# An attention kernel on one core: TensorE's instructions in the order of the text, and its side work dealt out by half steps

## The chip, the core and the metric

The kernel runs on one core of a Trainium2 chip. The metric is the time of one execution on the device, in microseconds. The core's engines work side by side: TensorE (PE in the profile) multiplies matrices, VectorE (DVE) and ScalarE (ACT) work on elements, GpSimd (POOL) here only issues transfers that gather or scatter rows, and SyncE (SP) issues the other transfers. Each engine takes its instructions strictly in the order in which the built program lists them, and waits where an operand or a buffer is not there.

## The reference, cut to what matters

For each of 16 sequences of 1024 tokens and 512 channels, the reference computes a self-attention with 8 heads of 64 channels, masked by tokens, and adds it to the input:

```python
q = xt @ Wq.T                                   # xt: tokens x channels
scores = 0.125 * einsum('bhqd,bhkd->bhqk', qh, qh)
logits = (scores * cmask + (1 - cmask) * NEG) * rmask
ctx = einsum('bhqk,bhkd->bhqd', softmax(logits), qh)
out = x + transpose(ctx @ Wo.T)
```

Query, key and value are the same projection `q`. A masked key gets no weight; a masked query attends to all tokens alike, so all its outputs are one row per sequence.

## The kernel before

**Tiling.** About half of the tokens of a sequence ("batch") are active. `slots` sorts the active ones to the front, `index` turns this into row numbers, and the kernel gathers C = 544 slots of each sequence: four tiles of 128 rows (`xa`) and one of 32 (`xt`). All matrices of a batch are made of these slots; the other rows only get the mean row (`rest`).

**Work of a batch**, by function:
- `xt` (L388): four transposes of a gathered tile into a tile of the pool `pm`; `xsplit` (L351) then splits it into two float16 halves, `xh` by ACT (L358) and `xl` by DVE (L359). Both read the `pm` tile.
- `query` (L411): 12 float16 matmuls into `pm`, ACT copies them to `q` (L424), and for the second half of the columns DVE masks the last ones (L427). `qsplit` makes the float16 pair `hl`, and SP spreads it to `xx`.
- `value` (L461) and `value_tail` (L473): transposes of `q`, copied by ACT to `v` and by DVE to `tmp`; `top` and `bottom` (L499, L513): the shift of the exponent of four heads.
- `scores` (L542): four float16 matmuls of 272 columns into a two-bank tile `pss` (L580), and one exponential by ACT (L584). With `i=None` it does the last 32 rows of four heads at once (L555).
- `attend` (L589): attention times value. Each of its four matmuls of float32 data has 64 output columns (L597); the two of a pair of heads use the left and right half of the array. `i=4` adds the last 32 keys (L600).
- `recip_sums`, `recip_rows`, `norm`: the division by the row sums. The sums go through a transpose (L633), a DRAM tile `rd` and back as `rb` before DVE multiplies (L664).
- `project` (L687) with `product` (L672): 12 matmuls of 512 columns (L680), DVE adds the input (L685), GpSimd scatters the rows (L764). `rest` gathers the other rows into `xi`, adds the mean on DVE (L751) and scatters them.

Most results of TensorE pass through `pm`, which has two buffers; `pss` has two as well, and `pav` (attend) one.

**The order of the work.** `run` goes through the batches `b`. A batch has 18 steps: for each of 4 pairs of heads-pairs `p` and row tiles `i` two `scores`, and twice the `scores` of the last rows. In the same steps the kernel does the side work of its neighbours: the queries and values of batch `b+1`, the projection of `b-1`, the indices and gathers of `b+2`. This side work is a list `m` of pairs (cost, function), and a share of it, `total / N`, follows the two scores of each step:

```python
                goal = total * (st + 1) / N
                while pos < len(m) and (done + m[pos][0] / 2 <= goal or st == N - 1):
```

`attend` for a step runs some steps later (`todo`, `ready`), when its exponentials are done. `post` keeps scatters and gathers in two lines, `urgent` and `spare`, of which `issue` takes one in each step; such a transfer also waits for `self.beat`, the matmul issued last at that place (`once`).

**Who sets the order within an engine.** The text names the work, but the Tile scheduler orders each engine's instructions when the program is built, by priorities and by its own estimate of what is ready. So the order on TensorE need not be that of the text: matmuls of one `attend` may stand apart, with transposes or scores between them. `tc.high_priority` raises some helpers, and `behind` ties instructions to one that must come first.

Of the kernel before, what the change touches and what calls it, by code (L numbers as in the profile page):

```python
# [10 lines left out]
F32 = mybir.dt.float32  # L11
# [8 lines left out]
P = 128  # L20
# [5 lines left out]
DC = D // P  # L26
# [23 lines left out]
class Fast:  # L50
# [114 lines left out]

    def slots(self, b0, b1):
# [7 lines left out]
        mb = self.sb([P, B, TB], F32, "sc", 3)  # L174
        nc.vector.tensor_scalar(mb, self.mt[:, bs], 0.5, None, ALU.is_gt)
        mh = self.sb([P, B, TB], F16, "tmp", 2)
        nc.vector.tensor_copy(mh, mb)
# [32 lines left out]
    def facts(self, b0, b1):  # L210

# [17 lines left out]
        eh = self.sb([P, B], F16, "tmp", 2)  # L229
        nc.vector.tensor_copy(eh, e)  # L230
        pe = self.pm([P, B])
        nc.tensor.matmul(pe, lhsT=self.on16, rhs=eh, start=True, stop=True)
# [3 lines left out]

    def index(self, b):
        nc = self.nc
        s = self.st[b]
        ol = self.sb([P, TB, P], F16, "tmp", 2)  # L240
        lo = self.lo[:, b]
        nc.vector.tensor_tensor(ol, self.io128.unsqueeze(1).broadcast_to([P, TB, P]),
                                lo.unsqueeze(2).broadcast_to([P, TB, P]), ALU.is_equal)
# [228 lines left out]

    def value_tail(self, b, g):  # L473
# [6 lines left out]
        q = self.sb([P, 2, HG, CT], F32, "qt")  # L480
        nc.scalar.copy(q, s["q"][:, 2 * g:2 * g + 2, 512:C].unsqueeze(2).broadcast_to([P, 2, HG, CT]))
# [13 lines left out]
    def shift(self, b, g):  # L495
        self.top(b, g)
        self.bottom(b, g)

    def top(self, b, g):  # L499

        nc, s = self.nc, self.st[b]
        hs = slice(HG * g, HG * g + HG)
        wide = self.smcol[g]
        sm = wide[:, :HG]
        nc.vector.tensor_reduce(sm.rearrange("p (e h) -> p e h", h=2),
                                s["sd"][:, 2 * g:2 * g + 2, :].rearrange("p e (k h) -> p e h k", h=2), AX.X, ALU.max)
        nc.vector.tensor_tensor(sm, sm, s["sdt"][:, hs], ALU.max)
        pt = self.pm([P, P])
        nc.tensor.transpose(pt, wide, self.ident)
        m = s["m"] = self.sb([P, 1], F32, "m", 2)  # L510
        nc.vector.tensor_reduce(m, pt, AX.X, ALU.max)
# [262 lines left out]
    def last(self, b, todo):  # L774
# [8 lines left out]
        self.recip(b, 3)  # L783
# [5 lines left out]
        for i in range(4):  # L789
            self.product(s["ch"], s["cl"], slice(i * P, (i + 1) * P), pos[i], range(3))  # L790
        self.norm(b, 3)
# [8 lines left out]
    def run(self, flag):  # L800
# [32 lines left out]
        for c in range(DC):  # L833
            self.load("q", c, 0)
        self.slots(0, 2)
        self.warm(36)
        self.index(0)
# [16 lines left out]
        def index1():  # L854
            with self.behind(self.last_xs):
                self.index(1)
# [11 lines left out]
        first += value(0, 1) + [(0, L(self.value_tail, 0, 0))] + query(0, 2, 0) + g1[2:3] + query(0, 2, 1)[:1] + g1[3:4]  # L868
# [7 lines left out]
        begin = g1[4:] + [(1.5, lambda: None)] + query(0, 3, 0) + value(0, 2) + query(0, 3, 1) + value(0, 3)  # L876
        begin += [(0.3, L(self.value_tail, 0, 1)), (0, L(self.means, 0))]
# [4 lines left out]
        for b in range(B + 1):  # L882
            o, n = b - 1, b + 1
            if b == B:
                self.last(o, todo)
                break
            free, early, late = {}, ([], []), []
            if b >= 1:
                early = [(0, L(self.recip_sums, o, 3))], [(0.1, L(self.recip_rows, o, 3))]
                late = [(0, L(self.norm, o, 3))]  # L890
            if n < B:
                if b in tails:
                    free[0] = [L(self.late, o, 4)]
                    late += [(2.6, L(self.project_tail, o))]
                for x in rests.get(b, []):
                    free.setdefault(0, []).extend(L(self.late, x, j) for j in range(5, 9))
                    late += [(0, L(self.rest, x, j)) for j in range(5, 9)]
            chunk2 = [(0, L(self.norm, o, 2))] if b else []
            P_ = (lambda *i: project(o, *i)) if b else (lambda *i: [])
            tp, bt = [(0.1, L(self.top, b, 1))], [(0.1, L(self.bottom, b, 1))]  # L900
            if n < B:
                m = xt(n)[:1] + early[0] + xt(n)[1:2] + chunk2 + xt(n)[2:3] + early[1] + xt(n)[3:] + tp + query(n, 0, 0) + query(n, 0, 1) + bt + value(n, 0)
                m += query(n, 1, 0) + late + P_(0) + query(n, 1, 1) + P_(1)
                m += [(0, L(self.range_x, n, c)) for c in range(DC)]
                r = P_(2) + value(n, 1) + [(0.25, L(self.value_tail, n, 0))] + query(n, 2, 0) + query(n, 2, 1)
                r += query(n, 3, 0) + [(0.1, L(self.top, n, 0))] + value(n, 2) + query(n, 3, 1)
                r += [(0.1, L(self.bottom, n, 0))] + P_(3) + value(n, 3)
                r += [(0.25, L(self.value_tail, n, 1)), (0, L(self.means, n))]
                if b + 2 < B:
                    m += [(0.5, L(self.index, b + 2))]  # L910
                    r[1:1] = [(0, L(self.gather, b + 2, j)) for j in range(5)]
                if b == 0:
                    for c in range(DC):
                        r.insert(1 + 3 * c, (0, L(self.split, "o", c)))
                m += r
            else:

                places = [("xi", 4), ("xa", 13)]
                come = [[L(self.late, x, j, *places[k % 2]) for j in range(5, 9)] for k, x in enumerate(rests[b])]
                leave = [[L(self.rest, x, j) for j in range(5, 9)] for x in rests[b]]  # L920
                free[0] = [L(self.late, b, 4)] + come[0]
                for c, l in zip(come[1:] + [[]], leave):
                    free[0] += c + l
                m = chunk2 + early[0] + early[1] + tp + bt + [(2.6, L(self.project_means, b))] + late + P_(0, 1, 2, 3)
            for g in groups:
                if b == g[0] - 1:
                    m.insert(7, (0.1, L(self.facts, *g)))
                if b == g[0] - 2:
                    m.insert(7 if b == 0 else 0, (0.1, L(self.slots, *g)))
            if b == 1:  # L930
                m.append((0, L(self.range_w, "o")))
            if b == B - 1:
                m.append((0.1, self.ranges))
            if b == 0:
                m = begin + m
            if b + 2 < B:
                self.start(b + 2)
                for c in range(DC):
                    at = 3 * c + (0 if b else 4)
                    free.setdefault(at, []).append(L(self.load_all, b + 2, c))  # L940
                    free.setdefault(at + 4, []).append(L(self.sum_half, b + 2, c))
            if b == 0:
                for k in range(3, 2 * DC):
                    free.setdefault(k // 2, []).append(L(self.sum_half, 1, k))
            total = sum(c for c, _ in m)
            done, pos = 0.0, 0
            for st, (p, i) in enumerate(S):
                soon, self.soon = self.soon, []
                for f in soon + free.get(st, []):
                    f()  # L950
                if i is None:
                    self.scores(b, p, None)
                else:
                    ps = [self.scores(b, 2 * p, i)]
                    if i == 2 and whole:
                        whole.pop()()
                    ps.append(self.scores(b, 2 * p + 1, i))

                for _ in range(1 if b < B - 2 else -(-len(self.urgent + self.spare) // (N - st))):
                    self.issue()  # L960
                goal = total * (st + 1) / N
                fill = []
                while pos < len(m) and (done + m[pos][0] / 2 <= goal or st == N - 1):
                    fill.append(m[pos])
                    done += m[pos][0]
                    pos += 1

                big = st >= 4 and [c >= 1 for c, _ in fill if c > 0.1][:1] == [True]
                fill = [f for _, f in fill]

                now = []
                if i in (0, 2):
                    ready, todo = todo, []
                elif i in (1, 3):
                    now, ready = ready, []
                for f in fill + now if big else now + fill:
                    f()
# [157 lines left out]
```

## Time and profile before

| what | us |
|---|---|
| median of 3 runs | 1136.92 (1134.63 to 1141.5) |
| the profiled execution | 1133.56 |
| its span, first to last instruction | 1131.8 |
| PE busy | 1090.5 |
| DVE busy | 731.6 |
| ACT busy | 676.2 |
| POOL busy | 289.1 |

The profiled execution's time is its span and 1.8 us around it. Busy times are sums over the span, and the end of a matmul is modelled, so a busy PE need not be streaming all the time; the distance from one matmul's start to the next one's start tells more. Of the span, about the first 100 us fill the pipeline (weights, first gathers) and the last 120 us empty it; between them each batch takes about 66 us.

### The profile page before, as it was taken

What the parts mean: (1) busy time and instruction counts of PE and PEld (TensorE: products, weight loads), DVE (VectorE), ACT (ScalarE), POOL (GpSimd) and SP (SyncE); (2) the same over time, 40 slices, a digit from 0 to 9 for tenths busy, and PEclk for the clock granted to TensorE, in tenths of its full rate; (3) what the DMA queues carried; (4) which work ended last, traced back from release to release, by engine and by line L of the source; (5) the groups of instructions that cost most, each with busy time, mean ns of one, the idle gap of its engine ahead of it and who ended that gap; (6) DMA issues with size and microseconds to landing.
All of it is one profiled execution on the core that took longest, in us unless ns stands there. A gap on an engine that the chain in (4) does not pass through costs nothing.

```text
span 1131.8 us, 23296 instructions
## 1 busy us (share of the span) xinstructions
PE 1090.5 (96%) x8386; PEld 707.9 (63%) x8386; DVE 731.6 (65%) x2369; ACT 676.2 (60%) x1716; POOL 289.1 (26%) x303
## 2 busy tenths in 40 slices
PE   7899999999999999999999999999999999998997
PEld 6566666666666666566666666566666666665543
DVE  6687567675665767667665666856576675655643
ACT  5776666666566666566565665666656566654540
POOL 3101021322202222222222232222222232214642
PEclk9899999999999999999999999999999999999999
DMA  6745554656546454655655566455655654545652
GB/s 212 218 117 151 143 159 128 191 142 179 149 127 175 124 201 137 171 175 158 189 150 165 154 177 185 129 181 144 195 166 156 188 152 130 149 126 174 204 161 77
DMA packets 78122, 181.35 MB, mean 160 GB/s; under 512 B 15008, under 2 KB 16800, under 8 KB 78000
## 3 DMA queue, kind: packets, MB, share of 16 engines
q1 hardware_dynamic: 56816, 111.62, 35.6%
q0 software_dynamic: 21184, 68.18, 18.7%
q8 instruction: 68, 1.11, 0.4%
q14 instruction: 54, 0.44, 0.1%
HBM read 92.34 MB, written 33.91 MB: 112 GB/s over the span
## 4 chain that ended last, share of the span: by engine, by line
PE 66%; DVE 14%; DMA 11%; issue 5%; ACT 2%; POOL 1%; SPq 1%; DVEq 0%; POOLq 0%; ACTq 0%
PE pav L597 19%; PE pss L580 16%; PE pm L680 13%; PE pm L421 8%; DMA rb<-rd 4%; PE pm L398 2%; DMA rd<-rr 2%; PE pav L600 2%; DMA xi<-x_in,idx 2%; PE pm L467 1%; DVE c L664 1%; DMA xx<-hl 1%; PE pm L633 1%; DVE tmp L458 1%; PE pss L555 1%
## 5 line engine op out<-in xcount | busy, mean ns | idle before, releaser
L584 ACT ACTIVATE p<-pss,nm 128x544 f32<-128x544 f32 x512 | 363.3, 714 | 231.5 <-PE pss L580 219.5
L580 PE MATMUL pss<-xx 128*128 128x272 f16 x2048 | 303.0, 281 | 4.2 <-DMA xx<-hl 2.7
L597 PE MATMUL pav<-p,v 128*64 128x272 f32 x2048 | 297.5, 402 | 0.9 <-ACT c L604 0.9
L580 PEld LDWEIGHTS <-xx 128*128 128x128 f16 x2048 | 192.1, 99 | 85.4 <-issue 41.2
L597 PEld LDWEIGHTS pav<-p,v 128*64 128x64 f32 x2048 | 140.6, 137 | 105.4 <-issue 40.9
L764 POOL DMA_INDIRECT y_out<-xa,idx x68 | 70.9, 1043 | 302.4 <-PE pss L580 163.6
L421 PE MATMUL pm<-xh,wqh 128*128 128x274 f16 (+1 forms) x512 | 143.9, 281 | 0.1
L421 PE MATMUL pm<-xl,wqh 128*128 128x274 f16 (+1 forms) x512 | 143.2, 280 | 0.2 <-DVE xl L359 0.2
L421 PE MATMUL pm<-xh,wql 128*128 128x274 f16 (+1 forms) x512 | 143.3, 280 | 0.0
L313 POOL DMA_INDIRECT xa<-x_in,idx x68 | 70.0, 1029 | 184.6 <-PE pss L580 89.3
L421 PEld LDWEIGHTS <-wqh 128*128 128x128 f16 x1024 | 99.9, 99 | 21.9 <-issue 3.4
L584 ACT ACTIVATION_READ_ACCUMULATOR p<-pss,nm 128x1 f32 x512 | 102.7, 201 | 0.0
L685 DVE SCALAR_TENSOR_TENSOR xa<-pm,xa 128x512 f32<-128x512 f32 x60 | 41.4, 689 | 89.6 <-PE pm L680 89.5
L313 POOL DMA_INDIRECT xi<-x_in,idx x60 | 59.6, 994 | 153.9 <-PE pss L555 53.9
L680 PE MATMUL pm<-woh,ch 128*128 128x512 f16 x240 | 91.0, 379 | 0.3 <-DVE ch L667 0.3
L680 PE MATMUL pm<-woh,cl 128*128 128x512 f16 x240 | 91.1, 379 | 0.1
L680 PE MATMUL pm<-wol,ch 128*128 128x512 f16 x240 | 91.0, 379 | 0.0
L424 ACT ACTIVATE q<-pm 128x272 f32<-128x272 f32 (+1 forms) x128 | 51.0, 398 | 64.0 <-PE pm L421 63.8
L764 POOL DMA_INDIRECT y_out<-xi,idx x60 | 60.9, 1015 | 92.0 <-PE pss L580 72.9
L664 DVE TENSOR_TENSOR c<-c,rb 128x544 f32<-128x544 f32 x64 | 46.2, 722 | 49.2 <-DMA rb<-rd 42.5
L680 PEld LDWEIGHTS <-ch 128*128 128x128 f16 x480 | 46.1, 98 | 41.0 <-DVE ch L667 0.8
L751 DVE TENSOR_TENSOR xi<-xi,ub 128x512 f32<-128x512 f32 (+1 forms) x60 | 40.1, 687 | 40.2 <-DMA xi<-x_in,idx 27.7
(191 smaller groups left out, 1585.5 us busy)
## 6 DMA issues: line engine op xcount, KB each, us to landing
xx<-hl SPq DMA_DIRECT2D x256, 136.0 KB
xm<-x_nat_in SPq DMA_DIRECT2D x56, 512.0 KB
rb<-rd SPq DMA_DIRECT2D x128, 136.0 KB
pt<-c SPq DMA_DIRECT2D x64, 136.0 KB
pt<-p SPq DMA_DIRECT2D x64, 136.0 KB
ub<-ud SPq DMA_DIRECT2D x16, 256.0 KB
xi<-x_nat_in SPq DMA_DIRECT2D x8, 256.0 KB
xa<-x_in,idx POOLq DMA_INDIRECT x68, 4.3
```

What stands on the lines that cost most here:

```text
L313: dma = self.nc.gpsimd.indirect_dma_start(out=tile[:n], out_offset=None, in_=self.x, in_offset=bass.IndirectOffsetOnAxis(ap=idx, axis=0))
L398: self.pe = nc.tensor.transpose(pt[:, c, :], x[:n, c * P:(c + 1) * P], self.ident[:n, :n]).ins
L421: self.beat = nc.tensor.matmul(pq, lhsT=w[:, c, e * P:(e + 1) * P], rhs=xx[:, c, cols], start=(k == 0), stop=(k == 3 * DC - 1)).ins
L424: nc.scalar.activation(s["q"][:, e, cols], pq, AF.Copy, scale=1.0 / (SX * SW))
L580: self.beat = nc.tensor.matmul(pt[:, g, :CH], lhsT=xx[:, 2 * k, i * P:(i + 1) * P], rhs=xx[:, 2 * k + a, g * CH:(g + 1) * CH], start=(a == ...
L584: self.exp = [nc.scalar.activation(t.rearrange("p (g c) -> p g c", g=2), pt[:, :, :CH], AF.Exp, bias=s["nm"][p // HG][:, p % HG:p % HG + 1 ...
L597: nc.tensor.matmul(s["pav"][k * DK:(k + 1) * DK, g, :CH], lhsT=s["v"][p][:, i, k * DK:(k + 1) * DK], rhs=ps[k][:, cols], start=(i == 0), s ...
L664: nc.vector.tensor_tensor(c, c, s["rb"][p], ALU.mult)
L680: nc.tensor.matmul(po[:cols.stop - cols.start], lhsT=a[:, e, cols], rhs=w[:, e, :], start=(e == 0 and k == 0), stop=(e == DC - 1 and k == 2))
L685: self.nc.vector.scalar_tensor_tensor(x, po, 1.0 / (SX * SW), x, ALU.mult, ALU.add)
L751: self.nc.vector.tensor_tensor(x[:n], x[:n], s["ub"][:n], ALU.add)
L764: dma = self.nc.gpsimd.indirect_dma_start(out=self.out, out_offset=bass.IndirectOffsetOnAxis(ap=idx, axis=0), in_=x, in_offset=None)
```

## The change

- The loop over batches stands in `manual_schedule` for TensorE: inside it, its instructions are issued as the text gives them. The other engines are still ordered by the scheduler.
- The side work is dealt out in shares. A step has up to two places for it: after its first `scores`, and at its end (after `attend`, where it has one). `share` gives the size of both, by the kind of step; before, all of it stood behind both `scores`.
- Helpers are cut in two, so that the part on DVE or ACT stands earlier than the part on TensorE that uses it: `active` from `slots`, `facts_sums` from `facts`, `hot` from `index`, `tail_copy` from `value_tail`, `peaks` from `top`. Three of them get a buffer of their own or another one.
- The list `m` is put in another order: `xt` tiles two by two, `index` earlier, `value` one query further from its own query, the gathers (`take`) behind the third projection. In the last batch, empty entries with a cost keep parts of the work apart.
- In `last`, the transpose of the last sums stands behind the first 9 matmuls of the projection.

```diff
+    def hot(self, b):
+        ol = self.st[b]["ol"] = self.sb([P, TB, P], F16, "tmp", 2)
...
+    def tail_copy(self, b, g):
+        q = s["qt"] = self.sb([P, 2, HG, CT], F32, "qt")
+        self.nc.scalar.copy(q, s["q"][:, 2 * g:2 * g + 2, 512:C].unsqueeze(2).broadcast_to([P, 2, HG, CT]))
...
     def shift(self, b, g):
+        self.peaks(b, g)
         self.top(b, g)
         self.bottom(b, g)
...
-        self.recip(b, 3)
+        self.recip_sums(b, 3)
...
         for i in range(4):
             self.product(s["ch"], s["cl"], slice(i * P, (i + 1) * P), pos[i], range(3))
+            if i == 0:
+                self.recip_rows(b, 3)
...
-        for b in range(B + 1):
...
+        with self.tc.manual_schedule(engines={self.nc.tensor.engine}):
+            for b in range(B + 1):
...
-                m = xt(n)[:1] + early[0] + xt(n)[1:2] + chunk2 + xt(n)[2:3] + early[1] + xt(n)[3:] + tp + query(n, 0, 0) + query(n, 0, 1) + bt + value(n, 0)
-                m += query(n, 1, 0) + late + P_(0) + query(n, 1, 1) + P_(1)
-                m += [(0, L(self.range_x, n, c)) for c in range(DC)]
-                r = P_(2) + value(n, 1) + [(0.25, L(self.value_tail, n, 0))] + query(n, 2, 0) + query(n, 2, 1)
-                r += query(n, 3, 0) + [(0.1, L(self.top, n, 0))] + value(n, 2) + query(n, 3, 1)
-                r += [(0.1, L(self.bottom, n, 0))] + P_(3) + value(n, 3)
-                r += [(0.25, L(self.value_tail, n, 1)), (0, L(self.means, n))]
+                    m = sums + pk(b, 1) + x[:2] + second + x[2:4] + rows + x[4:]
...
+                    m += q(0, 0) + tp(b, 1) + q(0, 1)
...
+                    m += bt(b, 1) + q(1, 0) + v(0) + third + q(1, 1)
...
+                    m += tc(0) + rng[:2] + tail + v(1) + P_(0) + tv(0) + rest + P_(1) + hot + rng[2:] + q(2, 0) + index
+                    m += pk(n, 0) + q(2, 1) + tp(n, 0) + P_(2) + take + v(2) + q(3, 0) + bt(n, 0)
+                    m += q(3, 1) + tc(1) + [(0, L(self.means, n))] + P_(3) + v(3) + tv(1)
...
+                share = [(1.2, 0) if i is None else ((0.95, 0.95), (0.9, 0), (0.45, 0.95), (0.9, 0))[i] for _, i in S]
+                unit = sum(c for c, _ in m) / sum(map(sum, share))
...
+                    fill(share[st][0], st == N - 1)
+                    if i is not None:
+                        ps.append(self.scores(b, 2 * p + 1, i))
...
+                    elif i in (1, 3):
+                        for f in ready:
+                            f()
+                        ready = []
+                    fill(share[st][1])
```

## The prediction

> **What bounds the kernel now.** I read the busy row first, then the groups, the windows, and TensorE's timeline.
>
> ```profile
> PE 1090.5 (96%) x8386; PEld 707.9 (63%) x8386; DVE 731.6 (65%) x2369; ACT 676.2 (60%) x1716; POOL 289.1 (26%) x303
> ...
> L580 PE MATMUL pss<-xx 128*128 128x272 f16 x2048 | 303.0, 281 | 4.2 <-DMA xx<-hl 2.7
> L597 PE MATMUL pav<-p,v 128*64 128x272 f32 x2048 | 297.5, 402 | 0.9 <-ACT c L604 0.9
> ```
>
> TensorE is the bound: 96% busy, and its dearest groups hardly wait. The windows (busy time of PE, PEld, DVE, ACT, POOL; granted clock; DMA share; GB/s) agree:
>
> ```profile
> 30.00:36.00 6.00, 3.33 (x26) 2.27 (x23) 4.07 (x9) 3.34 (x11) 1.89 (x2) 0.89 0.95 274
> 36.00:42.00 6.00, 5.53 (x28) 3.72 (x27) 3.56 (x15) 2.81 (x8) 0.00 (x0) 0.54 0.83 318
> 48.00:54.00 6.00, 4.46 (x40) 3.00 (x40) 4.80 (x14) 5.28 (x12) 0.00 (x0) 1.00 0.21 48
> 380.00:450.00 70.00, 69.09 (x534) 44.39 (x532) 47.38 (x164) 42.29 (x106) 18.16 (x18) 1.00 0.54 162
> ```
>
> In the steady part 69.09 of 70 us are busy, at full clock. So there is no large idle time to win; a gain must make the same matmuls cheaper. TensorE's timeline (start, length, line, output, count) shows how:
>
> ```profile
> 300.67 2.05 PE L597 MATMUL pav<-p,v 128*64 128x272 f32 x16
> 302.65 0.66 PE L467 MATMUL pm<-ident,q 128*128 128x128 f32 x4
> ...
> 306.61 0.67 PE L597 MATMUL pav<-p,v 128*64 128x272 f32 x2
> 307.21 0.66 PE L398 MATMUL pm<-ident,xa 128*128 128x128 f32 x4
> 307.80 0.68 PE L597 MATMUL pav<-p,v 128*64 128x272 f32 x4
> 308.41 0.33 PE L633 MATMUL pm<-ident,rcol 128*128 128x128 f32 x1
> ```
>
> Each float32 matmul leaves two records, so x16 is eight matmuls, or four pairs of left and right half of the array. From start to next start the eight take 1.98 us, one pair 0.61 and one lone half 0.60: **a half alone costs as much as a pair.** A pair is (1.98 - 0.61) / 3 = 0.458, leaving the half-array mode 0.153; the matmul that enters it starts 0.209 behind the one before, where 272 columns otherwise take 0.116: 0.093 for entry.
>
> **The gain on TensorE.** Counted in the built order, before has 198 unbroken stretches of L597, 44 of them a lone matmul, together 552 pair slots. After has 127 stretches, 126 of eight, 512 slots.
> - 40 slots x 0.458 = 18.3.
> - 71 stretches x (0.153 + 0.093) = 17.5.
> - 45 to 32 stretches of the last rows' scores, 13 x about 0.1, and 71 first intervals behind an exit, 0.02 each: 2.7.
>
> That is **38.5 us less**. No matmul is added.
>
> **The xt tiles, two by two.** `xt` transposes into `pm`, two buffers, and a tile is freed only when ACT (`xh`) and then DVE (`xl`) have read it.
>
> ```profile
> L358 ACT ACTIVATE xh<-pm x75: 272/597/645, 51.1 to 985.4; 128x512 f16<-128x512 f32 x60, 128x128 f16<-128x128 f32 x15
> ```
>
> ```profile
> L359 DVE SCALAR_TENSOR_TENSOR xl<-pm,xh x75: 279/681/693, 51.8 to 986.2; 128x512 f16<-128x512 f32 x60, 128x128 f16<-128x128 f32 x15
> ```
>
> (Columns: min/median/max ns.) Before, work of several us mostly stands between two tiles. After, 9 batches have scores, xt0, xt1, scores, xt2, xt3, `recip_rows`, xt4, scores, query; 5 have the second scores one tile later. With the first scores' first matmul at 0: the exponential ends at 1.36, xh0 at 1.96, xl0 at 2.67, so xt2 starts at 2.73, not 1.80 (+0.93). xl1 ends at 3.28: xt3 +0.17. xh2 stands behind the second exponential, xl2 ends at 4.68: `recip_rows` +0.96. xl3 at 5.29: xt4 +0.45. Sum 2.5 us. The other order gives 1.40 + 0 + 0.67 + 1.02 = 3.1. So 9 x 2.5 + 5 x 3.1 = **38.0 us more**. Below: if ACT and DVE serve the tiles sooner, or part of the stall would have come elsewhere, about half. Above: DVE is 65% busy, and one foreign operation of 0.7 us ahead of an `xl` in each batch adds 10.
>
> The Trainium skill speaks against this edit ("Perfetto Trace Analysis", Optimizing Tensor Performance, Matmuls): independent groups should rotate through PSUM banks, so that emptying one overlaps the next. Two banks do rotate, so by the rule alone this costs nothing (sum 1090); by the rows a tile needs 0.44 us of TensorE and about 2 us to come free, so two banks are too few and the sum is 1128. I take the rows.
>
> **Gathers later.** The gathers of `b+2` stand behind the third projection. Before, the last is released 10 to 26 us ahead of its use; after, by the order and the durations, only 1.1 us in 5 batches, 5 in 9. The matmul that a gather waits for is followed 0.55 later by GpSimd's start, and the landing comes 3.2 (median) after that:
>
> ```profile
> DMA to landing us min/median/max: 2.5/3.2/5.0
> ```
>
> The xt waits above lengthen the 1.1 to 3.7, which leaves about 0.4: 5 x 0.4 = **2 us more** (none if the xt waits are longer, 5 x 2.6 if they vanish, but then those 38 us are saved).
>
> **The waits between engines that go and come.** From start distances, before loses 25 us between 100 and 1010 us: `top`'s reduction on DVE ahead of a `recip_rows` 8.1 (11 times), exponential ahead of scores 4.6, the query's mask ahead of `value` 4.5, `value_tail`'s copy ahead of xt 3.0, `recip_sums` 1.8, smaller ones 3.0. The cut helpers and half-step shares take these away nearly whole, bound below by the few that return: `value` behind its mask 3.6, `query` behind `bottom` 2.0, `recip_sums` 2.8. A fourth is DVE's queue:
>
> ```profile
> DVE xi L751 <- DMA xi<-x_in,idx: 27.7, 20, 3.8
> ...
> DVE xi L751 <- DMA ub<-ud: 12.2, 5, 3.4
> ```
>
> These adds of `rest` wait 39.9 us at the head of DVE's queue, with `xl` and masks behind them, mostly harmless while TensorE had other work to issue. In the new order one such wait in ten hits an operation TensorE needs at once: 4 us. So 12.4 come, 25 go: **12.6 us less**. Ends: 0 and 20.
>
> **Clock.** The windows above show half clock (0.54) behind 30 to 36, in which PE was busy 3.33 of 6, and full clock behind 48 to 54, busy 4.46, mostly transposes. The Trainium skill ("TensorE: Matmul & The Clock Gate", Part 4) says that transposes don't count as busy in the same way, and Part 1 that one idle window of about 3.4 us halves the clock. By the rule each batch's xt chain, transposes and waits, would give such a window: 14 x 1.7 us (half of a window lost) = 24. The trace does not bear that out for transposes: in 48 to 54 the clock stayed at 1.00. Streaming shares near the observed limit (0.36 halved, 0.48 not) come in 2 or 3 batches: **3.4 us more**.
>
> **Ramp and tail.** At the start two xt tiles move ahead and the second spread of `xx` is read 3.2 us after the first scores: 2.5 more; the weights' range (2.27 us on DVE) no longer stands ahead of the first shift, which I count in it. In `last`, the last `recip_rows` stands behind 9 products, 9 x 3 x 0.216 = 5.8 us of work that covers most of the 7.75 us from there to `norm`; no net.
>
> **What costs nothing.** `active`, `facts_sums`, `hot`, `tail_copy`, `peaks` run the same instructions as before on DVE and ACT, with 35 and 40% free. SP issues the same transfers; its `xx` reads have at least 24 us in the steady part; GpSimd has 74% free. If a buffer of its own failed to cover, the wait is one DVE operation, 0.7 us in a batch, within the ends.
>
> **Sum,** against the profiled execution's own 1133.56 (span 1131.8 and 1.8 around it; the median shown is 3.4 above): 1133.56 - 38.5 + 38.0 + 2.0 - 12.6 + 3.4 + 2.5 = **1128.4**. I put down 1128.
>
> **Forecast, 0.42: the gain is eaten by the two buffers.** 1128, own range 1115 to 1141. For it: both counts rest on rows. Against: the chain assumes that ACT and DVE are never early or late.
>
> **Rival 1, 0.30: the xt chain costs half.** ACT's and DVE's order absorbs the later waits of a batch, and stalls that follow one another are counted once: 1128 - 19 = 1109, 1101 to 1122. For it: 40% of ACT is free. Against: the exponential stands ahead of xh in the order.
>
> **Rival 2, 0.20: DVE's adds at the head of the queue, slower.** Three quarters of the 39.9 us reach TensorE, because xt chains, masks and `value` have no lead left: 30 - 4 = 26 more, 1154. It makes the kernel slower than before from 5.2 us on (1133.56 - 1128.4), and by over 1% from 20 on. For it: the transfers that the adds wait for come no sooner. Against: the 25 waits average 1.6 us, and a queue that TensorE has left well ahead of need hides that.
>
> **Rival 3, 0.08: the clock halves in each batch,** 24 in place of 3.4: 1149. For it: the page's rule. Against: the row of 48 to 54.
>
> That the change does not do what it says is out: the built order has 126 stretches of eight.
>
> **Numbers.** About 1% is what a measurement of this kernel tells from no change: 1125.5 to 1148.3. Of the forecast a third lies below (0.14 faster, 0.28 same); rival 1 gives 0.28 and 0.02; rival 2 0.16 slower, 0.04 same; rival 3 0.05 and 0.03. Together faster 0.42, same 0.37, slower 0.21. The range 1104 to 1157 leaves out the lower end of rival 1 and the upper end of rival 2.
>
> **What would show it.** Right: L597's busy sum falls; nearly all its rows are x16; new rows "PE pm L420 <- DVE xl" of some 30 us, one to three waits in each batch of 0.2 to 1.4 us; steady batches of some 66 us, as before. Rival 1: the same rows under 20 us. Rival 2: DVE's waits for `xi` grow and TensorE waits for DVE lines behind L751's. Rival 3: a granted clock of 0.5 in every batch. I am wrong if the stretches of eight don't save what the distances say, or if the waits sit at other tiles than xt's.

## The result, and the profile after

The changed kernel takes 1206.17 us (median of 4, 1201.79 to 1210.56) where the kernel before, beside it, takes 1137.52: **slower, ratio 1.060, interval 1.054 to 1.066.** The profiled execution took 1209.73 us, 76.2 more than before's 1133.56; its span is 1208.0. The forecast was 1128, within a range of 1104 to 1157. It was wrong in size and in sign. One run of e12 below fell in a slower state of the chip; it is left out of that run's ratio, though not of its median.

The page, its busy row and two of its groups (busy, mean ns | idle before):

```profile
PE 1084.6 (90%) x8386; PEld 715.5 (59%) x8386; DVE 740.9 (61%) x2369; ACT 686.1 (57%) x1716; POOL 291.2 (24%) x303
...
L628 PE MATMUL pav<-p,v 128*64 128x272 f32 x2048 | 269.2, 406 | 0.0
```

L628 (L597 before) went from 297.5 us to 269.2 with the same matmuls, and yet TensorE is busy for 90% of a longer span instead of 96%. The gain is there, and idle time has eaten it. Next is the window of the steady part (after its length: busy time of PE, PEld, DVE, ACT and POOL, granted clock, DMA share, GB/s), to be set against before's 69.09 of 70:

```profile
380.00:450.00 70.00, 63.97 (x495) 42.63 (x495) 44.77 (x140) 40.63 (x103) 17.29 (x17) 0.98 0.54 158
```

Six of 70 us are now idle. The list of TensorE's waits (line waited for by which, us in total, times, longest):

```profile
PE pm L511 <- DVE xa L716: 19.2, 11, 4.9
PE pm L420 <- DVE xl L381: 17.8, 24, 1.8
PE pm L489 <- DVE q L449: 15.4, 8, 3.1
PE pm L664 <- DVE xl L381: 9.4, 14, 0.8
PE pm L443 <- DVE xa L716: 9.0, 5, 2.5
```

The second and fourth rows are the xt tiles, which the prediction had. The first and last are new: transposes and a query wait for a `pm` tile that the projection's add on DVE (`plus`, L716) has not yet emptied. The third is `value`, waiting for the query's mask.

To set kernels side by side I took, from each trace, the distance from each matmul's start to the next start, and subtracted what the same kind takes where nothing waits (the prediction's 0.116, 0.458, 0.153 and so on). What is left over is waiting; a wait over 0.15 us is put down to the instruction that ended within 0.17 us ahead of the late start. A row adds up to the time from the first matmul's start to the last one's. It is of one profiled execution, while the times of the experiments below are medians: the profiled execution was 3.6 us above its median in the changed kernel, 6 to 7 above in e3 and e14, and 4 below in the kernel before. Times in us:

| kernel | work | xt tiles | product's add | mask to `value` | other named waits | half clock | rest |
|---|---|---|---|---|---|---|---|
| before | 1051.9 | 4.0 | 0 | 8.1 | 25.1 | 4.9 | 25.9 |
| after | 1013.2 | 37.4 | 33.0 | 19.7 | 35.0 | 25.3 | 33.0 |
| e1 | 1013.2 | 20.4 | 39.1 | 5.3 | 32.5 | 11.7 | 30.5 |
| e2 | 1013.2 | 37.5 | 13.4 | 20.7 | 36.6 | 28.0 | 31.2 |
| e3 | 1042.8 | 0 | 39.0 | 18.5 | 21.1 | 16.4 | 30.9 |
| e4 | 1013.4 | 47.6 | 0.3 | 8.5 | 58.3 | 20.8 | 33.0 |
| e5 | 1013.2 | 19.8 | 12.8 | 5.2 | 31.4 | 13.2 | 31.1 |
| e7 | 1013.2 | 20.4 | 16.2 | 5.4 | 26.0 | 8.2 | 28.4 |
| e14 | 1013.2 | 36.5 | 50.3 | 5.4 | 39.2 | 20.4 | 42.0 |

(Other: row sums, shift, exponential, facts and slots. Half clock: what matmuls take longer while the clock is halved. Rest: short waits, and what the unit times miss. Where two instructions end together, the split between columns is rough, in e4 above all.) From before to after, work falls by 38.7 and waiting grows by 115.4.

### The profile page after: what moved, and what is told of

It is laid out like the page before. It is cut to its first block, busy times and chain, and to the rows that moved or that the text cites. A ratio compares the mean times of both kernels' runs of the same rounds, so it can differ in the third digit from the quotient of the medians.

```text
span 1208.0 us, 23368 instructions
## 1 busy us (share of the span) xinstructions
PE 1084.6 (90%) x8386; PEld 715.5 (59%) x8386; DVE 740.9 (61%) x2369; ACT 686.1 (57%) x1716; POOL 291.2 (24%) x303
## 3 DMA queue, kind: packets, MB, share of 16 engines
q1 hardware_dynamic: 56816, 111.62, 32.5%
## 5 line engine op out<-in xcount | busy, mean ns | idle before, releaser
L611 PE MATMUL pss<-xx 128*128 128x272 f16 x2048 | 321.3, 284 | 3.2 <-ACT p L615 2.6
L628 PE MATMUL pav<-p,v 128*64 128x272 f32 x2048 | 269.2, 406 | 0.0
L611 PEld LDWEIGHTS <-xx 128*128 128x128 f16 x2048 | 195.7, 101 | 78.7 <-issue 31.6
L628 PEld LDWEIGHTS pav<-p,v 128*64 128x64 f32 x2048 | 138.3, 139 | 98.8 <-issue 34.9
L795 POOL DMA_INDIRECT y_out<-xa,idx x68 | 67.9, 998 | 371.5 <-issue 115.9
L443 PE MATMUL pm<-xl,wqh 128*128 128x274 f16 (+1 forms) x512 | 145.8, 285 | 0.0
L695 DVE TENSOR_TENSOR c<-c,rb 128x544 f32<-128x544 f32 x64 | 46.4, 725 | 127.7 <-DMA rb<-rd 74.0
L443 PEld LDWEIGHTS <-wqh 128*128 128x128 f16 x1024 | 102.4, 101 | 37.6 <-issue 17.1
L335 POOL DMA_INDIRECT xa<-x_in,idx x68 | 67.3, 989 | 187.7 <-PE pss L611 79.1
L711 PE MATMUL pm<-woh,ch 128*128 128x512 f16 x240 | 94.1, 392 | 1.2 <-DVE xa L716 1.2
L711 PE MATMUL pm<-wol,ch 128*128 128x512 f16 x240 | 93.9, 391 | 0.0
L782 DVE TENSOR_TENSOR xi<-xi,ub 128x512 f32<-128x512 f32 (+1 forms) x60 | 40.3, 689 | 71.3 <-DMA xi<-x_in,idx 53.0
L489 PE MATMUL pm<-ident,q 128*128 128x128 f32 x256 | 44.1, 287 | 23.6 <-DVE q L449 15.4
```

The source lines that it names most:

```text
L335: dma = self.nc.gpsimd.indirect_dma_start(out=tile[:n], out_offset=None, in_=self.x, in_offset=bass.IndirectOffsetOnAxis(ap=idx, axis=0))
L443: self.beat = nc.tensor.matmul(pq, lhsT=w[:, c, e * P:(e + 1) * P], rhs=xx[:, c, cols], start=(k == 0), stop=(k == 3 * DC - 1)).ins
L489: nc.tensor.transpose(pv[:, k, :], s["q"][:, e, k * P:(k + 1) * P], self.ident)
L611: self.beat = nc.tensor.matmul(pt[:, g, :CH], lhsT=xx[:, 2 * k, i * P:(i + 1) * P], rhs=xx[:, 2 * k + a, g * CH:(g + 1) * CH], start=(a == ...
L628: nc.tensor.matmul(s["pav"][k * DK:(k + 1) * DK, g, :CH], lhsT=s["v"][p][:, i, k * DK:(k + 1) * DK], rhs=ps[k][:, cols], start=(i == 0), s ...
L695: nc.vector.tensor_tensor(c, c, s["rb"][p], ALU.mult)
```

## Where the waits come from, line by line

**The xt tiles.** TensorE's timeline after, one batch (idle before and its releaser in brackets):

```profile
246.16 1.25 PE L420 MATMUL pm<-ident,xa 128*128 128x128 f32 x8 [0.77 <-DVE xl L381]
248.23 0.33 PE L664 MATMUL pm<-ident,rcol 128*128 128x128 f32 x1 [0.82 <-DVE xl L381]
248.83 0.43 PE L420 MATMUL pm<-ident,xt 32*128 32x32 f32 x4 [0.27 <-DVE xl L381]
```

The eight are xt2 and xt3. The idle times 0.77, 0.82 and 0.27 stand in the places for which the prediction had 0.93, 0.96 and 0.45.

**The product's add.** TensorE's timeline after, at the end of a batch, and DVE's in the same time:

```profile
597.43 0.63 PE L611 MATMUL pss<-xx 128*128 128x272 f16 x4
597.89 0.60 PE L489 MATMUL pm<-ident,q 128*128 128x128 f32 x4
600.45 0.44 PE L511 MATMUL pm<-ident,qt 128*128 128x128 f32 x2 [1.96 <-DVE xa L716]
```

```profile
593.03 0.29 DVE L459 COPY hl<-hl 128x544 f16<-128x544 f16 x1
598.65 0.73 DVE L695 TENSOR_TENSOR c<-c,rb 128x544 f32<-128x544 f32 x1 [5.33 <-DMA rb<-rd]
599.41 0.39 DVE L696 SCALAR_TENSOR_TENSOR c<-nh,mq,c 128x160 f32<-128x160 f32 x1
599.71 0.68 DVE L716 SCALAR_TENSOR_TENSOR xa<-pm,xa 128x512 f32<-128x512 f32 x1
```

Read them together. The products gave way to scores at 597.4. Their add needs nothing else, but DVE has stood idle since 593.3 (593.03 + 0.29) at `norm` (L695), which waits 5.33 us for the row sums to come back from DRAM. This is the norm of head pair 2 (`second`), which the text has in the next batch; the scheduler, which still orders DVE, put it in front of the add. TensorE was not late because DVE was busy: **DVE was idle, with the wrong instruction at its head.**

**The mask.** The same thing; here adds of `rest` (L782), waiting for their gathers, stand in front of the mask (L449). TensorE and DVE after:

```profile
695.18 0.52 PE L489 MATMUL pm<-ident,q 128*128 128x128 f32 x3
698.61 0.43 PE L489 MATMUL pm<-ident,q 128*128 128x128 f32 x1 [2.90 <-DVE q L449]
```

```profile
694.25 0.69 DVE L782 TENSOR_TENSOR xi<-xi,ub 128x512 f32<-128x512 f32 x1 [3.05 <-DMA xi<-x_in,idx]
...
697.62 0.69 DVE L782 TENSOR_TENSOR xi<-xi,ub 128x512 f32<-128x512 f32 x1 [1.08 <-DMA xi<-x_in,idx]
698.23 0.32 DVE L449 TENSOR_TENSOR q<-q,hr 128x160 f32<-128x160 f32 x1
```

How much is each of the two? Going back from every late start in after's trace along DVE's order to the last wait for a transfer, I find `norm` behind 16 of the product's add's 33 us. The adds of `rest` stand behind 9 of that row, 13 of the masks' 19.7 (five waits) and 6 of other waits (two, for the facts): some 28 us in all. This is read from one trace; a late start can have more than one cause, and no run ties `rest`'s adds alone in the changed kernel. DVE's own waits at these instructions grew. The list of DVE's waits, for `norm` before and then for both after (for the adds before had 27.7 and 12.2 us):

```profile
DVE c L664 <- DMA rb<-rd: 42.5, 29, 3.7
```

```profile
DVE c L695 <- DMA rb<-rd: 74.0, 36, 7.1
DVE xi L782 <- DMA xi<-x_in,idx: 53.0, 28, 7.1
DVE xi L782 <- DMA ub<-ud: 12.6, 5, 3.2
```

**The clock.** Four windows after (the numbers behind POOL's count are granted clock, DMA share, GB/s):

```profile
309.50:312.90 3.40, 0.72 (x7) 0.48 (x4) 0.66 (x1) 1.28 (x3) 0.00 (x0) 1.00 0.84 241
312.90:319.70 6.80, 5.66 (x24) 2.81 (x25) 5.10 (x18) 1.45 (x4) 0.88 (x1) 0.51 0.04 10
531.40:534.80 3.40, 1.78 (x11) 0.98 (x9) 2.40 (x4) 2.56 (x6) 0.99 (x1) 1.00 0.19 77
534.80:538.20 3.40, 3.17 (x16) 2.27 (x17) 2.56 (x7) 1.08 (x3) 0.00 (x0) 0.51 0.11 31
```

A stretch with much waiting (0.72 or 1.78 us busy of 3.40) is followed by one at half clock. After has 18 such stretches, before 4.

## The experiments

**e1: the tiles apart.** `gap = [(0.85, lambda: None)] if b else []`, and in `m`:

```diff
-m = sums + pk(b, 1) + x[:2] + second + x[2:4] + rows + x[4:]
+m = sums + pk(b, 1) + x[:1] + gap + x[1:2] + gap + second + x[2:3] + gap + x[3:4] + rows + gap + x[4:]
```

> The changed kernel with one edit: empty entries of cost 0.85 between the xt tiles, so that each of the five stands in its own half step, mostly with 0.9 us or more of other TensorE work between two. TensorE's stretches of eight stay as they are. Theory (several waits, each of its own cause; the two pm buffers one of them): the 36 us that TensorE waits behind xsplit and behind the transposes between the tiles fall to about 12, one or two half-clock windows in three go with them, and the other waits stay: 1206 - 24 - 5 = about 1177 (1165 to 1188). Rival A (DVE's queue is late whatever stands on TensorE, the xt waits are only where it shows): the waits move to the next user, within 8 us of 1206. Rival B (the two buffers are nearly all of it): below 1145.

1166.57 us, ratio 1.021 (1.014 to 1.029): 40 less, inside the theory's range, but more than all of the tiles' waits. Those fell by 17, the masks' by 14, half clock by 14, while the product's add grew by 6. That needed e12 to e14.

**e2: the norm behind.** `last_xs` is the `xl` of the second tile; `behind` sets only the order on DVE:

```diff
-second = [(0, L(self.norm, o, 2))] if b else []
+def norm2(o=o):
+    with self.behind(self.last_xs):
+        self.norm(o, 2)
+second = [(0, norm2)] if b else []
```

> The changed kernel with one edit: the norm of head pair 2 is queued on DVE behind the xl of the second xt tile (issue order only, no wait), where the text has it; in the changed kernel the scheduler put it in front of the last product's add of the batch before. Theory: DVE then no longer stands at that norm's row sums with the product's add behind it, and the 17 us in 14 waits of value_tail for that add vanish: 1206 - 17 and up to 4 for the clock, about 1187 (1180 to 1195). Rival A (DVE is simply full at the end of a batch): under 5 us. Rival B (the wait for the row sums moves to the next operation in DVE's queue, an xl of the xt tiles): within 6 us of 1206 with the xt waits longer.

1195.86 us, ratio 1.049 (1.043 to 1.056): 10 less, just short of the theory's range. The waits for the product's add fell by 20 as the theory has it, and DVE's for `rb` from 74.0 to 23.9 us. By the medians the kernel kept half of the 20; by the profiled executions it kept 15, with masks, other waits and half clock each some more.

**e3 and e4: order and text apart.** e3 is the changed kernel without `manual_schedule`; e4 is the kernel before with its loop inside it:

```diff
 e3
-        with self.tc.manual_schedule(engines={self.nc.tensor.engine}):
+        if True:
 e4
-        for b in range(B + 1):
+        with self.tc.manual_schedule(engines={self.nc.tensor.engine}):
+            for b in range(B + 1):
```

> The changed kernel's text, helpers and shares, but TensorE's order left to the scheduler as before. By the built order the stretches of L628 fall back to 191, 40 of them lone, and TensorE's work without waits is 30 us more than in the changed kernel (9 less than before). Theory (the order of the text on TensorE alone, against DVE's order by the scheduler, makes the waits): they shrink to near before's, about 1130 to 1150. Rival (the new places of the helpers and shares make the waits): about as slow as the changed kernel or slower, 1190 to 1240.

> The kernel before, only with TensorE's instructions in the order of its text; list, shares and helpers as before. The built order has 128 stretches of L628, all of eight, so TensorE's work without waits is 38 us less than before, as in the changed kernel; but three xt tiles stand in a row and two more, and each helper directly ahead of its own use. Theory: the gain of 38 is outweighed by waits, more of them than in the changed kernel, since nothing was moved to cover them: 1210 to 1260. Rival (what costs is the new list and the half steps): the gain shows, 1100 to 1130.

e3: 1176.26 us, ratio 1.032 (1.028 to 1.036). e4: 1196.37 us, ratio 1.052 (1.048 to 1.055). Neither theory nor rival had the number. In e3 the tiles' waits are gone, but the product's add costs 39 us, somewhat more than in the changed kernel: that wait comes with the new list and DVE's order under it, not with TensorE's order. In e4 the product's add costs nothing, but the tiles and the exponentials of the scores together about 70: the text's order alone brings those. So both halves of the change cost time, at different places, and the 38 us of work saved are in e4 as well.

**e5: e1 and e2 together.**

> The changed kernel with the edits of e1_xt_apart (tiles apart by empty entries) and e2_norm_behind (norm of head pair 2 behind the xl of the second tile) together. In e1's trace 23 us of TensorE's waits for a product's add are held at that norm. Theory (separate causes that add): e1 less 23 us, 1166 - 23 = about 1143 (1133 to 1153). Rival A (what is freed at DVE is taken by the next operation in its queue): above 1157. Rival B (the two edits overlap, e2's gain of 10 is all there is): 1153 to 1160.

1139.3 us, ratio 1.0017 (1.0003 to 1.0031): as expected, though the edits do not simply add: e2's is worth 10 us alone and 27 on top of e1. Together two small edits take away 67 of the 69 us. The waits of e5 (those rows are to be set against the five above):

```profile
PE pm L420 <- DVE xl L381: 6.1, 15, 1.8
PE pm L443 <- DVE xl L381: 5.4, 14, 0.4
PE pm L443 <- DVE xa L716: 4.9, 10, 1.5
PE pm L549 <- DVE n L192: 4.8, 4, 3.5
PE pm L511 <- DVE xa L716: 4.4, 1, 4.4
```

L511's 11 waits for the add are one, and L664 and L489 are no longer near the top.

**e6: DVE by the text as well.** On top of e1:

```diff
-        with self.tc.manual_schedule(engines={self.nc.tensor.engine}):
+        with self.tc.manual_schedule(engines={self.nc.tensor.engine, self.nc.vector.engine}):
```

> e1_xt_apart with DVE, too, in the order of the text, as TensorE is (manual_schedule for both engines). Theory (the scheduler's order on DVE, made by its own estimate of what is ready, is what puts norms, the adds of rest and top's reduction ahead of the product's add and of query's mask): the waits for product adds and masks, 39 and 5 us in e1, go nearly whole, about 1125 (1112 to 1140). Rival (in the text, too, norm, the row sums and the adds stand at places where DVE waits for transfers or for ACT; the scheduler at least passes some of them): the waits stay or grow, 1160 to 1210.

1237.72 us, ratio 1.088 (1.084 to 1.091): the rival's side, and beyond its range. The text is a worse order for DVE here than the scheduler's: the tiles cost 51 us, the row sums 39. Naming one wrong pair of instructions was worth more than taking the whole order.

**e7 and e11: rest's adds.** In `add` of `rest`, with `last_plus` the instruction of L716; e7 has it on top of e5, e11 alone on the kernel before:

```diff
-            self.nc.vector.tensor_tensor(x[:n], x[:n], s["ub"][:n], ALU.add)
+            with self.behind(self.last_plus):
+                self.nc.vector.tensor_tensor(x[:n], x[:n], s["ub"][:n], ALU.add)
```

> e5_apart_and_norm with one more edit: each of rest's adds is queued on DVE behind the product's add traced last, so that it no longer stands with its wait for the gather ahead of a query's mask. Theory: some 5 to 10 us of the waits for masks and product adds go, e5 less 5 to 10, about 1136. Rival 2 of the prediction (these adds are the large item): e5 less 20 or more. Rival (they are harmless): within 3 us of e5.

> The kernel before, with e7's last edit alone: rest's adds on DVE behind the product's add traced last. TensorE's order stays the scheduler's (198 stretches). Theory (before, DVE's waits at the head of its queue are hidden, since TensorE has other work ahead of the operations behind them; they cost only in the changed order): within 4 us of before. Rival (they cost before, too, and e7's 7 us have nothing to do with the order on TensorE): 5 us or more faster than before.

e7: 1132.2 us, ratio 0.995 (0.994 to 0.997), 7 less than e5 as the theory has it, but not where it said: the masks' waits stayed (5.2 and 5.4) and the product's add's grew (12.8 to 16.2), while half clock and other waits each fell by 5. e11: 1130.95 us, ratio 0.996 (0.994 to 0.998), 4.5 less, between the theory (within 4) and its rival (5 or more). Both beat the kernel before by half a per cent. So the adds cost a little in either of these orders. That is not their price in the changed kernel: e1's edit, which e7 contains, had already taken 14 of the masks' 19.7 us.

**e8: does the clock cost by itself?** In `scores` for the second head of each batch's first step:

```diff
+        if 0 < b < self.B - 1 and (p, i) == (1, 0):
+            for _ in range(16):
+                nc.tensor.matmul(pt[:, 0, :P], lhsT=self.on16, rhs=self.on16, start=True, stop=True)
```

> The changed kernel with one edit: in each of the 14 steady batches 16 dummy matmuls of 128 columns (about 0.9 us of streaming, their result overwritten) ahead of the second scores, which stand between xt1 and xt2; there TensorE otherwise waits about that long for the pm buffer. No dependency is moved, so this asks what the half-clock stretches cost by themselves. Theory (the waits starve the clock's window, and the clock is a cost of its own on top of them): the wait of xt2 shrinks by what the dummies take, the 18 half-clock stretches fall to 10 or fewer, 5 to 12 us less: about 1197 (1190 to 1202). Rival A (the clock is set by something else, or the dummies only fill time that was lost anyway): within 4 us of 1206. Rival B (TensorE was late by less than 0.9 us at this place, the dummies come on top): 1210 to 1220.

1209.23 us, ratio 1.061 (1.056 to 1.066), 18 half-clock stretches as before the edit: rival A. The tiles' waits shrank by 10, about what the dummies take. Which waits precede the changed kernel's stretches explains it: of the 17 ahead of its end only 3 follow the tiles; the others follow single long waits for an add, a mask or the facts, and those at start and end. The dummies stood at the wrong place, so what the clock costs by itself stays open. Stretches are fewer in kernels with fewer waits (18 in after, 10 in e1 and e5, 6 in e7), but not in step with them: e2 has 18 as well.

**e9 and e10: the rest of the tiles' waits.** Both on top of e7:

```diff
-second + x[2:3] + gap + x[3:4] + rows + gap + x[4:]
+second + x[2:3] + gap + rows + x[3:] + gap                                # e9
+second + x[2:] + (gap and [(0.5, lambda: None)]) + rows + gap             # e10
...
+                if 0 < b < B - 1:                                         # e10
+                    share[1] = 0.45, 0.8
```

> e7_rest_behind with the xt tiles and the rows' transposes placed by how long a pm buffer is held: the sums' transposes (recip_rows) between the third and the fourth tile's half steps, the short fifth tile directly behind the fourth, and an empty entry between it and the first query. Theory (the rest of the xt chain, 20 us in e7, is held by these places): half of it goes, e7 less 8 to 12, about 1122 (1116 to 1128). Rival (the waits move to the query or the scores): within 4 us of e7, 1128 to 1136.

> e7_rest_behind with the last two xt tiles ahead of the scores of the last 32 rows and the rows' transposes behind them, with scores before the first query; so no xl stands on DVE behind those scores' split (L595), which held the query in e9. In e7's trace the xt chain still costs 20 us, in e9's 33, of which 19 are held at that split. Theory (what holds an xl in DVE's queue decides, and this is the last such place of size): the chain falls from 20 to about 8, e7 less 10 to 14, about 1121 (1115 to 1127). Rival (TensorE is as full as it gets, the waits move on): 1128 or more.

e9: 1153.37 us, ratio 1.015 (1.012 to 1.017). e10: 1142.94 us, ratio 1.009 (1.006 to 1.011). Both misses. e9's DVE shows why; the last two `xl` (x2) stand behind the split of the last rows' scores (L595, L596), which waits for ACT:

```profile
314.31 0.52 DVE L595 CAST c<-p 128x544 fp32r<-128x544 f32 x1 [0.37 <-ACT p L590]
314.75 0.29 DVE L655 TENSOR_TENSOR rcol<-zt,corr 32x1 f32<-32x1 f32 x2
315.08 0.72 DVE L596 TENSOR_TENSOR p<-p,c 128x544 fp32r<-128x544 f32 x1
315.72 0.88 DVE L381 SCALAR_TENSOR_TENSOR xl<-pm,xh 128x512 f16<-128x512 f32 x2
```

e10 avoided that, but the rows' transposes then waited for an `xl` (11 us), and a query for the add, which stood on DVE behind `top`'s reduction (12 us). Each new place met another neighbour on DVE.

**e12 to e14: what e1's 40 us are.** All three keep the tiles together, but give all work behind them the later places that e1's empty entries give. e13 also moves the gathers (`take`) ahead; e14 leaves them and issues two transfers in each of a batch's last four steps.

```diff
-m = sums + pk(b, 1) + x[:2] + second + x[2:4] + rows + x[4:]
+m = sums + pk(b, 1) + x[:2] + second + x[2:4] + rows + x[4:] + 4 * gap                                   # e12
+m = sums + pk(b, 1) + x[:2] + (gap and [(0.4, lambda: None)]) + second + x[2:4] + rows + x[4:] + 3 * gap # e13, e14 (gap 1.0)
...
-m += pk(n, 0) + q(2, 1) + tp(n, 0) + P_(2) + take + v(2) + q(3, 0) + bt(n, 0)
+m += pk(n, 0) + take + q(2, 1) + tp(n, 0) + P_(2) + v(2) + q(3, 0) + bt(n, 0)                            # e13
...
-for _ in range(1 if b < B - 2 else
+for _ in range(2 if 0 < b < B - 2 and st >= N - 4 else 1 if b < B - 2 else                               # e14
```

> The changed kernel with the four empty entries of e1_xt_apart all behind the last xt tile. From the first query on, TensorE's order is e1's; the tiles stay together (three and two, as in 5 of the changed kernel's 14 steady batches). This parts e1's 40 us: in its trace only 17 of them are waits behind the tiles, 14 are waits for query's mask. Theory (both count: the spacing of the tiles, and the later places that the empty entries give to all that follows): the waits for masks fall as in e1 (14 us), the tiles' waits stay at 37 to 43, about 1190 (1182 to 1197). Rival A (the spacing is all of it): 1203 to 1212. Rival B (the later places are all of it): under 1175.

> As e12_entries_without_spacing, but with the tiles two, two and one as in 9 of the changed kernel's batches (an entry of 0.4 behind the second, three of 1.0 behind the last), and the gathers of b+2 one query and one projection sooner in the list; in e12 the empty entries had made the last gather so late that TensorE waited 22 us for it. From the first query on TensorE's order is e1's. Theory (e1's 40 us are partly the tiles' spacing and partly the later places of what follows): masks' waits stay at about 5, no waits for gathers, the tiles' waits about 37: 1206 - 14 and up to 5 for the clock, about 1190 (1184 to 1197). Rival A (the spacing is all of it): 1202 or more. Rival B (the later places are nearly all): under 1178.

> As e13_pairs_kept_gather_ahead, but with the list's gathers where the changed kernel has them, and two transfers in place of one issued in each of the last four steps of a batch; by the built order the last gather is then released 9 us of TensorE's work ahead of its use, where it had 0.7 in e12. The tiles stand two, two and one; from the first query on TensorE's order is e1's. Theory (e1's 40 us are partly the spacing of the tiles, partly the later places of what follows): no wait for a gather of size, masks' waits about 5 us, the tiles' about 37, 1190 (1184 to 1197), so the spacing is worth about 23 us. Rival A (the spacing is all of it): 1202 or more. Rival B (the later places are nearly all): under 1178.

e12: 1218.94 us, ratio 1.070 (1.068 to 1.073). That is outside all three forecasts. The first row of its waits is new, so it could not tell:

```profile
PE pm L420 <- DMA xt<-x_in,idx: 22.4, 14, 1.7
```

e13: 1271.42 us, ratio 1.120 (1.118 to 1.123), slower still. GpSimd's timeline in e13:

```profile
384.15 0.96 POOL L335 DMA_INDIRECT xa<-x_in,idx  x1 [1.64 <-PE pss L586]
401.07 0.99 POOL L795 DMA_INDIRECT y_out<-xa,idx  x1 [15.97 <-DVE tmp L480]
404.07 0.97 POOL L335 DMA_INDIRECT xa<-x_in,idx  x1 [2.01 <-DMA y_out<-xa,idx]
```

Three gathers went out sooner, but the fourth stands behind a scatter that comes 16 us later and frees its buffer: over the whole run TensorE then waited 50 us for `xa`. So the gathers cannot simply move ahead of the third projection.

e14: 1213.84 us, ratio 1.064 (1.059 to 1.070): no gather is waited for to any size, the masks cost 5 us as in e1 and the tiles 36.5, and the kernel is no faster than the changed one. That is rival A: with the later places but without the spacing, nothing of e1's 40 us is left, and e1 is 47 us faster than e14. Only 16 of these are the tiles' own waits (36.5 to 20.4); the product's add (50.3 to 39.1), the half clock (20.4 to 11.7) and other waits (39.2 to 32.5) are smaller in e1 as well. The masks' 14 us, which e14 does save, are outweighed by 17 more at the add. One thing is left untested: e14 also issues transfers in pairs, and what that costs by itself no run shows, so 47 may be too much for the spacing.

## Why the prediction was wrong

The profiled execution was to become 5 us faster and became 76 slower. By the table, the first matmul's start to the last one's grew by 76.7: -38.7 of work, +33.4 for the tiles, +54.5 for other named waits, +20.4 of half clock, +7.1 of rest.

- **The gain on TensorE** (38.5): right. The work fell by 38.7, and L628 is in stretches of eight.
- **The xt tiles** (38.0): right in place and size, 33.4 more than before (37.4 against 4.0). The row was the right side to take against the Trainium skill's rule of rotating through banks ("Perfetto Trace Analysis", Optimizing Tensor Performance, Matmuls), by which these waits would have been nothing. What the sum left out is what goes with these waits elsewhere: e1 is 47 us faster than e14, three times the tiles' own difference.
- **The gathers** (2): no size in the changed kernel; its list of waits has some 3 us for `xa`. In e12, where the lead was 0.7 us by the order, TensorE waited 1.6 us in each batch (22.4 in 14).
- **The waits that go and come** (-12.6): **this step failed.** It let before's 25 us go and 12.4 come. The named waits other than the tiles' are 33.2 before and 87.7 after: +54.5. The step "a fourth is DVE's queue" looked at one kind of instruction, `rest`'s adds, and let one of their waits in ten reach TensorE, 4 us. In after's trace they stand in front of some 28 us of TensorE's waits, of 65.6 that they wait themselves (53.0 and 12.6). And the product's add, 33 us, stood nowhere in the sum: in front of it stood `norm`, with its wait for `rb`, in before's trace at 42.5 us and in after's at 74.0; e2, which moves only this norm, takes 20 of the 33 away. I read the order on TensorE and not what it meets on DVE.
- **The clock** (3.4): +20.4, also too small. The Trainium skill's rule ("TensorE: Matmul & The Clock Gate", Part 1: an idle window of about 3.4 us halves the clock) came nearer with its 24, but the windows here were only partly idle: the 17 stretches ahead of the end follow windows of 3.4 us with about 2.1 to 3.4 us of waiting. Most of these are long waits that the sum had not foreseen. Whether transposes count as work for the clock no run here settles.
- **Rivals.** Rival 2 (1154) is nearest in mechanism: DVE's queue held by an instruction that waits for a transfer. Both of its signs came: DVE's waits for `xi` grew from 27.7 to 53.0 us, and TensorE waited for lines behind L782. Its 30 us for `rest`'s adds are close to the 28 read from after; it lacked `norm` and the further cost of clock and tiles. The share of `rest`'s adds is read from the trace, not shown by a run. Rival 3's 24 us of clock nearly came, as a consequence of the waits. Rival 1 has nothing for it.

## What to carry to other kernels

When one engine's order is fixed by hand and another's is left to a scheduler, read the second one's queue at each place where the first waits: look not for busy time but for an idle engine whose next instruction waits for something slow, and tie just that instruction behind the one that is needed. Tiles side by side on a pool of two need other work between them: each holds its buffer for about 2.4 us, so by an estimate from the prediction's 0.44 and 2 us one can start every 1.2 us, which leaves some 0.8 us for other work; e1's entries gave about that. The count of work saved held within a microsecond here. The counts of waits did not: removing the tiles' waits brought more than their sum (e1), removing the add's less (e2), since each wait moves others.

## What the runs showed of the hardware that was not expected

After's half-clock stretches follow windows of 3.4 us in which TensorE waited for about 2.1 to 3.4 us, also where the rest of the window held transposes (0.87 us of them ahead of 534.8, 893.2 and 968.3 us). The limit is not sharp by this reckoning: in after and e1 windows with up to 2.2 us of waiting kept full clock, in e8 some with 1.7 did not. As an estimate from the excess in them, one stretch costs about 1.4 us (25.3 / 18), so a single wait of 2 to 3 us for an add or a mask that brings one on costs about half as much again.
